# One projection for B, C and the step sizes, and state 2's product with B on GpSimd with its decay in PSUM, in a selective-scan kernel

## The chip, the cores and the metric

The kernel runs on one core of a Trainium2 chip. The metric is the device time of one execution in microseconds (us). A core has five engines that run side by side, each through its own list of instructions in order: TensorE (PE in the profile, its weight loads PEld), VectorE (DVE), ScalarE (ACT), GpSimd (POOL) and SyncE (SP), which here only issues the transfers (DMA) between the memory (HBM) and the on-chip memory (SBUF). PSUM is the second on-chip memory, into which TensorE writes its results.

## The reference

A network of four layers works on four images of 64 x 64 points with 96 channels. Each layer is a token mixer followed by a small feed-forward part in 8-bit floats. Layer 0 has a gated scan of its own; the change does not touch it. Layers 1 to 3 have a mixer that is a selective scan over four orders of the points (rows and columns, forward and backward). With 192 inner channels and 16 states, its core is

```python
delta = softplus(dt_proj(x_dbl[:6]) + dt_bias)      # step sizes
B, C = x_dbl[6:22], x_dbl[22:38]                    # x_dbl = x_proj_weight @ u
dA = exp(delta * A)                                 # decay, A = -(1..16)
h = dA * h + (delta * u) * B                        # for each channel and state, along the 4096 points
y = sum over states of h * C  (+ u * D)
```

All of it is fp32 in the reference.

## The kernel before, in words

**Tiling.** A stage is one image in one layer; layers 1 to 3 with four images make 12 stages, run by `scans`. A stage goes through two directions, four segments of T = 1024 points each, and three chunks of 128 rows (64 channels of one order and 64 of another): 24 chunks, 288 in all. Each chunk has 16 tiles, one for each state, so there are 4608 tiles of 128 x 1024 fp32. A tile is one round of the loop `for k in range(last + 5)`.

**A tile's work.** The decay `da` is an exponential on ScalarE (`decays`), two rounds ahead, in one of three SBUF buffers. The B rows of the state come onto all 128 partitions by two bf16 matmuls with a selection matrix (`b_rows`), one round ahead, in one of two PSUM buffers `bc` (two banks each, from `wide`). `scan` multiplies them by `du` = delta * u on VectorE, in place in PSUM, lets some side work be issued (`beside`), and runs the recurrence on VectorE as one scan instruction into one of three `h` buffers. One round later GpSimd multiplies `h` by the C rows (`times_c`, the result in `c`). Three rounds later TensorE adds the result to the chunk's sum in PSUM (`accumulate`). The C rows come from a small array `cs` in HBM: `c_rows` issues two transfers of 256 KB, each one row spread over 64 partitions, two rounds ahead, into one of six `c` buffers. A buffer is free again when its accumulation is done.

**A segment's preparation** (`next_segment`, `prepare_segment`). The inputs `u` are loaded, and then a projection gives B, C and the six inputs of the step size for two orders at once. The columns of its weights `xp` are B three times over (NB3 = 96), the step inputs (12) and C (32): XPW = 140, more than the 128 partitions of a result. So it is made in two passes, `x_proj_b` (108 rows) and `x_proj_c` (32 rows), each in two halves of 512 points and of three matmuls a half. B is kept as a sum of three bf16 parts in `bs`: the first part is a rounded copy, a VectorE subtraction gives the remainder, ScalarE rounds that, and GpSimd takes the last difference. That is why B stands three times in the projection: each part lies on partitions of its own. The C rows are copied out and stored to `cs`.

**A chunk's preparation** (`prepare_chunk`). While a chunk's 16 tiles run, the next chunk's step sizes are made: matmuls, then a softplus out of ScalarE tables and three GpSimd operations of 128 x 1024, and a fourth on GpSimd for `du`.

**What sets the order.** Every engine runs its instructions in the order in which the program issues them (class `InOrder`); waits between engines are put in from the data's dependences and from buffers that come free. The preparations are Python generators (`Chain`), and each round's `beside` moves each one step on. With one step in each round, and with the chunk's chain begun at state 0, the softplus operations on GpSimd are issued in the rounds of states 5, 8, 11 and 13. Two PSUM banks are shared by the chains and the side job.

**The side job.** The work between two stages (feed-forward, normalisation, the input projection, the 3 x 3 convolution of the next image) is a `Job` whose chains advance by `rate` steps a round, and which is finished by force, if need be, in the second last chunk of the stage at state 4, tile 356 of the stage's 384, where the next stage's first segment begins to load.

```python
            if k + 2 <= last:
                c_rows(k + 2)
                decays(k + 2)
            if n == 11:
                logarithms()
            if k + 1 <= last:
                b_rows(k + 1)
            if 0 <= k - 1 <= last:
                times_c(k - 1)
            if k <= last:
                scan(k, beside)
```

Of the kernel before, what the change touches and what calls it, by code (L numbers as in the profile page):

```python
# [23 lines left out]
R = 6  # L24
HID = 4 * C
# [14 lines left out]
XPW = NB3 + 2 * R + NC2  # L40
# [59 lines left out]
def metaformer(ctx: ExitStack, tc: tile.TileContext, x, l0_ab, l0_rest, ssm, ffn, out):  # L100
# [662 lines left out]
    def load_segment(item):  # L763
# [8 lines left out]
        sg.cs = dram.tile([NC2, T], F32, tag="cs", name="cs")  # L772
        return sg

    def prepare_segment(item, sg):

        xp = weights[item.layer].xp
        m = NB3 + 2 * R

        def project(ps, a, b, k):  # L780

            for c in range(3):
                o = (3 * item.d + c) * XPW
                cols = slice(k * MM, (k + 1) * MM)
                pe.matmul(
                    ps[0 : b - a],
                    xp[:, o + a : o + b],
                    sg.us[c][:, cols],
                    start=c == 0,
                    stop=c == 2,  # L790
                )
                if c:
                    yield

        sg.rows = sb(1, "rows", [128, T])
        for k in range(2):
            cols = slice(k * MM, (k + 1) * MM)
            ps = bank("x_proj_b")
            yield from project(ps, 0, m, k)

            bs = sg.bs[:, cols]
            act.copy(sg.rows[NB3:m, cols], ps[NB3:m])
            sg.steps = k == 1
            act.copy(bs, ps[0:NB3])
            yield
            rem = sg.rows[0:NB3, cols]
            dve.tensor_tensor(rem, ps[0:NB3], bs, ALU.subtract)
            release()
            yield
            for p in (32, 64):  # L810
                act.copy(bs[p : p + 32], rem[p : p + 32])
            yield k == 0
        pool.tensor_tensor(sg.bs[64:96], sg.rows[64:96], sg.bs[64:96], ALU.subtract)
        for k in range(2):
            cols = slice(k * MM, (k + 1) * MM)
            yield True
            ps = bank("x_proj_c")
            yield from project(ps, m, m + NC2, k)
            act.copy(sg.rows[0:NC2, cols], ps[0:NC2])
            release()  # L820
        yield
        sp.dma_start(out=sg.cs, in_=sg.rows[0:NC2])
# [50 lines left out]
    def scans(stages, jobs, pac):  # L873
# [27 lines left out]
        def c_rows(k):  # L901
            i, n = tiles[k]
            c = live[k, "c"] = sb(6, "c", [128, T])
            for half in range(2):
                row = NS * half + n
                sp.dma_start(
                    out=c[64 * half : 64 * half + 64],
                    in_=i.sg.cs[row : row + 1, :].to_broadcast([64, T]),
                )

        def decays(k):
            i, n = tiles[k]
            da = live[k, "da"] = sb(3, "da", [128, T])
# [80 lines left out]
        start(items[0])  # L994
        c_rows(0)
# [449 lines left out]
```

## Time and profile before

| what | value |
|---|---|
| time, median of 3 runs | 19,610.84 us (19,587.28 to 19,634.19) |
| the profiled execution's own time | 19,605.71 us |
| its span, first to last instruction | 19,603.9 us |
| VectorE busy | 17,669.3 us (90%) |
| TensorE busy | 16,279.3 us (83%), granted clock 0.816 |
| GpSimd busy | 15,496.4 us (79%) |
| ScalarE busy | 12,248.8 us (62%) |
| transfers (queue 1) | 3178 MB, 61.6% of the 16 DMA engines' time |
| scan, 128 x 1024, x4608 | 2343 ns each |
| VectorE product `bc<-du,bc`, x4608 | 1208 ns each |
| GpSimd product `c<-h,c`, 128 x 1024, x4608 | 2360 ns each |
| selection matmul `bc<-bs,sel`, x9216 | 457 ns each |
| second projection pass `x_proj_c`, x1152 | 687 ns each |
| row load `c<-cs`, 256 KB, x9216 | 4.2 us from issue to landing |

In a line of groups, the first part is line, engine and operation, then what is written and read (by the program's names) and how often; after it the busy time in us and the mean of one in ns; last the idle time of the engine just before these instructions, and what ended most of it. Nearly every instruction has the line L78, since a helper records them all; so groups go by the names of the tiles. In a list of waits each line says who waited for whom, for how long in total, how often, and the longest. In a list in order of time, the first two numbers are the start and the duration in us. An fp32 matmul leaves two records, a bf16 one leaves one.

### The profile page before, as it was taken

The page shows a single profiled execution, that of the slowest core. Times are in us where ns is not written, and L with a number is a line of the kernel's source. Part 1 is how long each engine was busy: PE and PEld are TensorE (multiplying, and loading weights), DVE is VectorE, ACT ScalarE, POOL GpSimd, SP SyncE. Part 2 cuts the span into 40 slices and gives each one's busy share as a digit, 9 for nine tenths or more (in the row PEclk, how much of TensorE's full clock was granted, in tenths as well). Part 3 has the DMA queues.
Part 4 walks back from the last instruction along what each step waited for, and adds up shares of the span by engine and source line. Part 5 has one row for each costly group of instructions (what it writes and reads, how often), then busy time and mean ns, then how long its engine had stood idle before and what let it go on. Part 6 is the DMA issues. An engine that isn't in the chain of part 4 may idle for free. (4 is left out here: it accounts for less than half of the span.)

```text
span 19603.9 us, 224830 instructions
## 1 busy us (share of the span) xinstructions
PE 16279.3 (83%) x70400; PEld 4745.4 (24%) x70400; DVE 17669.3 (90%) x13768; ACT 12248.8 (62%) x19341; POOL 15496.4 (79%) x10086
## 2 busy tenths in 40 slices
PE   8998787787888888887888887887888888888877
PEld 3332121121122222222222222222222222223223
DVE  6757999999999999999999999999999999998885
ACT  4544665665665665675665665665675665666665
POOL 3435888888888888888888888888888888888886
PEclk9998786787787787797797797797797797797776
DMA  2213666676666666667666667666666666676664
GB/s 52 50 47 89 166 184 168 168 188 166 169 186 172 170 182 180 167 185 182 169 183 180 167 182 183 167 182 182 168 186 178 168 185 176 171 185 171 168 177 115
DMA packets 1269876, 3192.65 MB, mean 163 GB/s; under 512 B 440336, under 2 KB 440560, under 8 KB 1262544
## 3 DMA queue, kind: packets, MB, share of 16 engines
q1 hardware_dynamic: 1268688, 3178.27, 61.6%
q8 instruction: 568, 9.31, 0.2%
q14 instruction: 620, 5.08, 0.1%
HBM read 2818.81 MB, written 308.28 MB: 160 GB/s over the span
## 5 line engine op out<-in xcount | busy, mean ns | idle before, releaser
L78 POOL TENSOR_TENSOR c<-h,c 128x1024 f32<-128x1024 f32 (+1 forms) x4992 | 11332.9, 2276 | 3284.9 <-DVE h L78 1396.4
L78 DVE TENSOR_TENSOR_SCAN h<-da,carry,bc 128x1024 f32<-128x1024 f32 x4608 | 10797.5, 2343 | 598.7 <-POOL c L78 80.8
L78 PE MATMUL acc<-c,twice 64*64 64x512 f32 x36864 | 6246.6, 755 | 57.4 <-POOL c L78 57.4
L78 ACT ACTIVATE da<-delta,decay 128x1024 f32<-128x1024 f32 x4608 | 5280.8, 1148 | 1372.5 <-DVE h L78 1359.7
L78 DVE TENSOR_TENSOR bc<-du,bc 128x1024 f32<-128x1024 f32 x4608 | 5567.1, 1208 | 417.8 <-PE bc L78 389.6
L78 PE MATMUL bc<-bs,sel 96*128 96x512 bf16 x9216 | 3398.6, 457 | 2393.3 <-DVE h L78 2296.6
L78 ACT COPY carry<-h 128x1 f32<-128x1 f32 x3456 | 649.1, 188 | 2997.7 <-DVE h L78 2992.8
L78 PEld LDWEIGHTS <-sel 96*128 96x128 bf16 x9216 | 557.0, 101 | 7376.4 <-DVE h L78 5607.2
L78 PEld LDWEIGHTS acc<-c,twice 64*64 64x64 f32 x36864 | 1131.3, 153 | 2848.4 <-issue 1927.6
L78 ACT ACT_TABLE_LOAD x1165 | 1494.7, 1283 | 36.3 <-DVE mv L78 20.0
L78 PE MATMUL conv<-pad,tap_lo 128*128 128x512 f32 x1728 | 913.5, 639 | 0.6 <-ACT zh L78 0.6
L78 PE MATMUL dt_proj<-rows,w 12*128 12x512 f32 x1152 | 829.5, 807 | 6.3 <-ACT delta L78 6.3
L78 ACT ACTIVATE du<-e,ones 128x1024 f32<-128x1024 f32 x576 | 659.4, 1145 | 202.9 <-POOL delta L78 197.8
L78 POOL TENSOR_TENSOR delta<-delta,du 128x1024 f32<-128x1024 f32 x288 | 679.2, 2358 | 121.7 <-ACT du L78 121.3
L78 PE MATMUL x_proj_c<-u,xp 128*32 128x512 f32 x1152 | 657.8, 687 | 133.2 <-ACT rows L78 125.0
L78 PE MATMUL x_proj_b<-u,xp 128*108 128x512 f32 x1152 | 696.1, 722 | 53.7 <-ACT u L78 12.8
L78 ACT COPY y<-acc 128x1024 f32<-128x1024 f32 x288 | 291.3, 1012 | 713.8 <-PE acc L78 708.9
L78 POOL TENSOR_TENSOR e<-e,du 128x1024 f32<-128x1024 f32 x288 | 679.7, 2360 | 2.4 <-ACT du L78 2.4
L78 POOL TENSOR_TENSOR du<-delta,u 128x1024 f32<-128x1024 f32 x288 | 680.0, 2361 | 0.1
L78 POOL TENSOR_TENSOR delta<-delta,e 128x1024 f32<-128x1024 f32 x288 | 678.7, 2357 | 0.1
L78 ACT ACTIVATE c<-c,l_bias 128x512 f32<-128x512 f32 x384 | 263.6, 686 | 662.6 <-PE c L78 659.8
L78 PE MATMUL conv<-pad,tap_hi 128*128 128x512 f32 (+1 forms) x1152 | 598.8, 621 | 3.8 <-ACT u L78 3.8
(152 smaller groups left out, 15323.9 us busy)
## 6 DMA issues: line engine op xcount, KB each, us to landing
c<-cs SPq DMA_DIRECT2D x9216, 256.0 KB, 4.2
u<-u SPq DMA_DIRECT2D x288, 512.0 KB, 6.8
y<-y SPq DMA_DIRECT2D x1152, 128.0 KB, 3.5
y<-y SPq DMA_DIRECT2D x144, 512.0 KB, 6.4
xr<-x SPq DMA_DIRECT2D x224, 192.0 KB, 5.1
u<-u SPq DMA_DIRECT2D x288, 128.0 KB, 2.7
pad<-y SPq DMA_DIRECT2D x288, 128.0 KB, 5.1
z<-zl SPq DMA_DIRECT2D x96, 256.0 KB, 3.4
```

The costliest lines, as they stand in the source:

```text
L78: ins = f(*a, **k).ins
```

## The change

- The projection has one pass of 108 columns: B once (32), C (32), 32 columns of zeros, and the step inputs (12). One copy brings all rows to SBUF; the remainder of B goes where the zeros were (partitions 64 to 95), and both later parts are rounded from there. `cs` now holds B and C, 64 rows.
- For the tiles of state 2 (`ON_POOL`), the B rows are loaded from `cs` by two transfers into a `c` buffer (`pool_rows`, four rounds ahead), and GpSimd multiplies them by `du` (`times_b`, issued two rounds ahead, in the round of state 0). VectorE has only the scan for that tile, and TensorE no selection matmul.
- The decay of these tiles is written into a PSUM buffer `bc`, one round ahead instead of two.
- The side job's rate is 1.6 steps a round instead of 1.65.

```diff
+ON_POOL = (2,)
...
-XPW = NB3 + 2 * R + NC2
+XPW = NB3 + 2 * R
...
     def prepare_segment(item, sg):
...
+        rows = sg.rows = sb(1, "rows", [128, T])
+        for k in range(2):
+            cols = slice(k * MM, (k + 1) * MM)
+            ps = bank("x_proj")
             for c in range(3):
                 o = (3 * item.d + c) * XPW
                 pe.matmul(
+                    ps[0:XPW], xp[:, o : o + XPW], sg.us[c][:, cols], start=c == 0, stop=c == 2
                 )
                 if c:
                     yield
...
-            act.copy(sg.rows[NB3:m, cols], ps[NB3:m])
+            act.copy(rows[0:XPW, cols], ps[0:XPW])
             sg.steps = k == 1
-            act.copy(bs, ps[0:NB3])
-            yield
-            rem = sg.rows[0:NB3, cols]
-            dve.tensor_tensor(rem, ps[0:NB3], bs, ALU.subtract)
+            act.copy(bs[0:32], ps[0:32])
+            yield
+            rem = rows[64:96, cols]
+            dve.tensor_tensor(rem, ps[0:32], bs[0:32], ALU.subtract)
             release()
             yield
             for p in (32, 64):
-                act.copy(bs[p : p + 32], rem[p : p + 32])
+                act.copy(bs[p : p + 32], rem)
             yield k == 0
-        pool.tensor_tensor(sg.bs[64:96], sg.rows[64:96], sg.bs[64:96], ALU.subtract)
-        for k in range(2):
-            cols = slice(k * MM, (k + 1) * MM)
-            yield True
-            ps = bank("x_proj_c")
-            yield from project(ps, m, m + NC2, k)
-            act.copy(sg.rows[0:NC2, cols], ps[0:NC2])
-            release()
-        yield
-        sp.dma_start(out=sg.cs, in_=sg.rows[0:NC2])
+        sp.dma_start(out=sg.cs, in_=rows[0 : 2 * NC2])
+        pool.tensor_tensor(sg.bs[64:96], rows[64:96], sg.bs[64:96], ALU.subtract)
...
+        def from_rows(i, dst, at):
+
             for half in range(2):
-                row = NS * half + n
+                row = NS * half + at
                 sp.dma_start(
-                    out=c[64 * half : 64 * half + 64],
+                    out=dst[64 * half : 64 * half + 64],
                     in_=i.sg.cs[row : row + 1, :].to_broadcast([64, T]),
                 )
...
+        def on_pool(k):
+            return k <= last and tiles[k][1] in ON_POOL
+
+        def pool_rows(k):
+            i, n = tiles[k]
+            b = live[k, "b"] = sb(6, "c", [128, T])
+            from_rows(i, b, n)
+
+        def times_b(k):
+            i, b = tiles[k][0], live[k, "b"]
+            pool.tensor_tensor(b, i.du, b, ALU.mult)
...
-            da = live[k, "da"] = sb(3, "da", [128, T])
+            da = live[k, "da"] = wide() if on_pool(k) else sb(3, "da", [128, T])
...
-            dve.tensor_tensor(b, i.du, b, ALU.mult)
+            if not on_pool(k):
+                dve.tensor_tensor(b, i.du, b, ALU.mult)
             beside()
...
             if k + 2 <= last:
                 c_rows(k + 2)
-                decays(k + 2)
+                if not on_pool(k + 2):
+                    decays(k + 2)
+            if on_pool(k + 1):
+                decays(k + 1)
+            if on_pool(k + 4):
+                pool_rows(k + 4)
             if n == 11:
                 logarithms()
-            if k + 1 <= last:
+            if k + 1 <= last and not on_pool(k + 1):
                 b_rows(k + 1)
             if 0 <= k - 1 <= last:
                 times_c(k - 1)
+            if on_pool(k + 2):
+                times_b(k + 2)
             if k <= last:
                 scan(k, beside)
...
-                jobs[-1].append(Job(between(im, layer - 1), 1.65))
+                jobs[-1].append(Job(between(im, layer - 1), 1.6))
...
-                for s in range(3):
-                    v[:, 32 * s + NS * order : 32 * s + NS * order + NS] = t[:, R : R + NS]
+                v[:, NS * order : NS * order + NS] = t[:, R : R + NS]
+                v[:, NC2 + NS * order : NC2 + NS * order + NS] = t[:, R + NS :]
                 v[:, NB3 + R * order : NB3 + R * order + R] = t[:, :R]
-                v[:, m + NS * order : m + NS * order + NS] = t[:, R + NS :]
```

More of the change, by code (lines that the diff above doesn't have):

```diff
@@ L771, in load_segment @@
         sg.bs = sb(2, "bs", [NB3, T], BF16)
-        sg.cs = dram.tile([NC2, T], F32, tag="cs", name="cs")
+        sg.cs = dram.tile([2 * NC2, T], F32, tag="cs", name="cs")
         return sg
@@ L777, in prepare_segment @@
         xp = weights[item.layer].xp
-        m = NB3 + 2 * R
-        def project(ps, a, b, k):
+        rows = sg.rows = sb(1, "rows", [128, T])
+        for k in range(2):
+            cols = slice(k * MM, (k + 1) * MM)
+            ps = bank("x_proj")
             for c in range(3):
                 o = (3 * item.d + c) * XPW
-                cols = slice(k * MM, (k + 1) * MM)
                 pe.matmul(
[L786 to L790, printed above, removed]
+                    ps[0:XPW], xp[:, o : o + XPW], sg.us[c][:, cols], start=c == 0, stop=c == 2
                 )
@@ L793, in project @@
                     yield
-        sg.rows = sb(1, "rows", [128, T])
-        for k in range(2):
-            cols = slice(k * MM, (k + 1) * MM)
-            ps = bank("x_proj_b")
-            yield from project(ps, 0, m, k)
             bs = sg.bs[:, cols]
-            act.copy(sg.rows[NB3:m, cols], ps[NB3:m])
+            act.copy(rows[0:XPW, cols], ps[0:XPW])
             sg.steps = k == 1
-            act.copy(bs, ps[0:NB3])
+            act.copy(bs[0:32], ps[0:32])
             yield
-            rem = sg.rows[0:NB3, cols]
-            dve.tensor_tensor(rem, ps[0:NB3], bs, ALU.subtract)
+            rem = rows[64:96, cols]
+            dve.tensor_tensor(rem, ps[0:32], bs[0:32], ALU.subtract)
             release()
@@ L810, in prepare_segment @@
             for p in (32, 64):
-                act.copy(bs[p : p + 32], rem[p : p + 32])
+                act.copy(bs[p : p + 32], rem)
             yield k == 0
-        pool.tensor_tensor(sg.bs[64:96], sg.rows[64:96], sg.bs[64:96], ALU.subtract)
-        for k in range(2):
-            cols = slice(k * MM, (k + 1) * MM)
-            yield True
-            ps = bank("x_proj_c")
-            yield from project(ps, m, m + NC2, k)
-            act.copy(sg.rows[0:NC2, cols], ps[0:NC2])
-            release()
-        yield
-        sp.dma_start(out=sg.cs, in_=sg.rows[0:NC2])
+        sp.dma_start(out=sg.cs, in_=rows[0 : 2 * NC2])
+        pool.tensor_tensor(sg.bs[64:96], rows[64:96], sg.bs[64:96], ALU.subtract)
     def prepare_chunk(item):
@@ L903, in c_rows @@
             c = live[k, "c"] = sb(6, "c", [128, T])
+            from_rows(i, c, NC2 + n)
+        def from_rows(i, dst, at):
             for half in range(2):
-                row = NS * half + n
+                row = NS * half + at
                 sp.dma_start(
-                    out=c[64 * half : 64 * half + 64],
+                    out=dst[64 * half : 64 * half + 64],
                     in_=i.sg.cs[row : row + 1, :].to_broadcast([64, T]),
                 )
+        def on_pool(k):
[7 more added lines that the diff above has]
+            pool.tensor_tensor(b, i.du, b, ALU.mult)
         def decays(k):
             i, n = tiles[k]
-            da = live[k, "da"] = sb(3, "da", [128, T])
+            da = live[k, "da"] = wide() if on_pool(k) else sb(3, "da", [128, T])
             at = (3 * i.d + i.chunk) * NS + n
@@ L994, in scans @@
         start(items[0])
+        for k in range(4):
+            if on_pool(k):
+                pool_rows(k)
+        for k in range(2):
+            if on_pool(k):
+                times_b(k)
         c_rows(0)
@@ L1365, in _scan @@
     xp = np.zeros((128, 2, 3, XPW), np.float32)
-    m = NB3 + 2 * R
     for d in range(2):
```

## The prediction

> **What bounds the kernel now.** I read the page first: busy shares, then the groups, then waits by engine, then single instructions in order of time.
>
> ```profile
> PE 16279.3 (83%) x70400; PEld 4745.4 (24%) x70400; DVE 17669.3 (90%) x13768; ACT 12248.8 (62%) x19341; POOL 15496.4 (79%) x10086
> ...
> L78 POOL TENSOR_TENSOR c<-h,c 128x1024 f32<-128x1024 f32 (+1 forms) x4992 | 11332.9, 2276 | 3284.9 <-DVE h L78 1396.4
> L78 DVE TENSOR_TENSOR_SCAN h<-da,carry,bc 128x1024 f32<-128x1024 f32 x4608 | 10797.5, 2343 | 598.7 <-POOL c L78 80.8
> ...
> L78 DVE TENSOR_TENSOR bc<-du,bc 128x1024 f32<-128x1024 f32 x4608 | 5567.1, 1208 | 417.8 <-PE bc L78 389.6
> ```
>
> VectorE is fullest. 4608 tiles (288 chunks of 16 states) each cost it one product with B and one scan. The list in order of time, in a quiet stretch of the sixth stage, gives the rhythm (start, duration, engine, what):
>
> ```profile
> 9005.56 1.21 DVE L78 TENSOR_TENSOR bc<-du,bc 128x1024 f32<-128x1024 f32 x1
> ...
> 9006.67 1.99 PE L78 MATMUL acc<-c,twice 64*64 64x512 f32 x8
> 9006.90 2.35 DVE L78 TENSOR_TENSOR_SCAN h<-da,carry,bc 128x1024 f32<-128x1024 f32 x1
> 9009.16 1.21 DVE L78 TENSOR_TENSOR bc<-du,bc 128x1024 f32<-128x1024 f32 x1
> 9009.28 1.15 ACT L78 ACTIVATE da<-delta,decay 128x1024 f32<-128x1024 f32 x1 [2.45 <-DVE h L78]
> ...
> 9009.38 2.37 POOL L78 TENSOR_TENSOR c<-h,c 128x1024 f32<-128x1024 f32 x1 [1.25 <-DVE h L78]
> ```
>
> Product to product is 3.60 us: 1.34 from the product's start to the scan's, 2.26 from there to the next product. The median of all 4607 intervals is 3.604, so most tiles run at VectorE's own pace. The products and scans run from 1802 to 19388 us, 17,585 us in all; 4607 x 3.603 = 16,599 of that. The other 986 are the projections' and the side job's VectorE work and real waits. Who VectorE waited for in that stretch:
>
> ```profile
> DVE bc L78 <- PE bc L78: 389.6, 271, 5.1
> DVE h L78 <- POOL c L78: 80.8, 36, 12.5
> DVE x L78 <- PE out_proj L78: 31.0, 20, 2.9
> ```
>
> Its idle time there is 1116 us, of which 599 is the 0.13 between product and scan; real waits are some 517, mostly for TensorE's B rows. GpSimd is busy 14,969 of the 17,585 us, 85.1%. And the SyncE queue:
>
> ```profile
> SPq L78 <- PE acc L78: 9566.6, 3839, 23.0
> ...
> POOL c L78 <- DMA c<-cs: 295.3, 80, 13.6
> ```
>
> The first line: the load of the C rows of a tile waits for the accumulation that frees one of the six "c" buffers. The second: GpSimd sometimes waits for those rows.
>
> **What the Trainium skill says.** "SBUF — State Buffer", section "Who interferes with whom": a VectorE instruction with two SBUF inputs locks out a GpSimd one that reads SBUF; with at most one it doesn't. The trace agrees for one: scans (decay in SBUF, B in PSUM) take 2.31 to 2.35 us from the 1st to the 99th percentile with GpSimd 85% busy beside them. With B in SBUF, the decay in PSUM keeps it at one, so I add no lock. "PSUM — Partial Sum Buffer", "The four PSUM rules": GpSimd cannot touch PSUM; hence B must come to SBUF by DMA for GpSimd's product. "GPSIMD Engine Reference", 3.1: a two-input fp32 product is 1.96 times as slow as on VectorE; here 2360/1208 = 1.95. "ScalarE: Activation LUTs", "Step-by-step", says writing PSUM has the lower latency; no run here shows a decay written there, so I take 1.15 us as now.
>
> **The change part by part** (against the profiled 19,605.7 us: span 19,603.9 and 1.8 around it).
>
> *State 2's product leaves VectorE.* Its tile then costs the scan's 2.26 us in place of 3.60: 288 x 1.34 = **-386 us**. The scan's inputs trade places between SBUF and PSUM, one of each as before, so its duration stays at 2343 ns; were its start 0.07 us worse or better, that is 20 us either way.
>
> *The same product comes to GpSimd:* 288 x 2.36 = 680 us. Share: (14,969 + 680)/(17,585 - 386) = 91%, so it isn't the bound on average; what counts is where it lands. It is issued in the round of state 0, after the previous state 15's product with C. I measured how far GpSimd is from holding up VectorE: a scan needs the "h" buffer of three scans ago, so the margin is from the end of the product with C of tile k to the start of scan k+3. Its median is 5.97 us for states 0 to 4, with a 5th percentile of 4.9 to 5.7 for states 0 to 3, but 0.64 and 0.04 at states 4 and 5. The four softplus sums run in the rounds of states 5, 8, 11 and 13. A delay of 2.36 fits into the 5.97 and is worked off at some 1.2 us a tile (3.60 - 2.36) before state 5, less the job's work and the 1.34 by which state 2's tile is shorter. What rides through to states 4 and 5 costs VectorE directly.
>
> *Its B rows come by DMA:* two issues of 256 KB for each chunk, 576 beside 9216. On SyncE they stand after state 0's C rows and before state 1's, and take one of the six "c" buffers from the round of state 14 to scan 2. The rows wait for the accumulation of state 11, which ends 11.1 us (median) after its own scan; with 0.1 to issue, 0.54 for the second half and 4.3 to land, they are there at 16.0, and GpSimd turns to them at about 16.8. At the 95th percentile they are 0.6 late, while scan 2 would wait only from some 2.5 us of lateness: some 8 us in sum over the 288. Behind them C rows of states 1 to 4 have five buffers instead of six, so they are issued 3 to 5 us later. I put that delay on each one's margin from landing to use (medians 5.4 to 6.9 now): 0 to 0.3 us is left at the 10th percentile of the worst states, and the shorter tile takes up to 1.34 more. So GpSimd will wait 0.5 to 1.5 us in perhaps a third of these tiles. VectorE sees this only where GpSimd is already late (states 4 and 5): I take **+70 us** for this and the product together; between 0 (all inside the 5.97) and 220 (some 0.75 us a chunk).
>
> *The decay goes to PSUM, and is issued one round later,* behind the decay of state 3. From the trace: its end would be 1.20 us (median) before scan 2 needs it; late in 16 of 288 chunks, 5.4 us in sum: **+5**. It takes a "bc" buffer that the B rows of state 2 no longer need, freed by the same scan.
>
> *State 2's selection matmuls go:* 576 x 0.457 us of TensorE, and VectorE's idle time ahead of these products, 20 us in the trace: **-20**.
>
> *One projection:* the C half goes (1152 matmul records, 657.8 us busy), with its two copies of 560 ns and a chain of six steps, which held one of two spare PSUM banks twice; the copy of 12 rows becomes one of 108 (as long: 579 against 582 ns for 96). VectorE's remainder stays one instruction of 677 ns. It runs in the third chunk of a segment; there VectorE's idle time before products of states 4 to 9 is 170 us, against 70 and 33 in the other two chunks. Half of the difference to their mean (170 - 52 = 118): **-60**; between 0 (the side job fills the place) and -120. The row store doubles to 256 KB but leaves some six rounds earlier; nobody waits for it.
>
> *The job's rate 1.65 to 1.6.* The job's last store falls at tile 339 of a stage's 384 (347 in the two that start a layer): 339 x 1.65 = 559 rounds, 347 x 1.65 = 573. At 1.6 they end at tiles 350 and 358; at 356 the kernel finishes a job by force and loads the next segment, whose rows then wait on SyncE for the stores. Two stages of nine can meet that: **+10**, at most 60.
>
> Sum: -386 + 70 + 5 - 20 - 60 + 10 = -381; 19,605.7 - 381 = 19,225. The median of the runs is 19,610.8, 5 above the profiled one: **19,230 us**, 1.9% less.
>
> **The rivals.**
> *Half is given back* (23%): the late C rows make GpSimd late at states 4 and 5, where the softplus sums begin and VectorE already stalls in 5% of chunks. For it: margins of 0.04 to 0.64 there, and GpSimd at 91%. Against: GpSimd's lateness there comes from waits, and extra work ahead of a wait disappears in it. At 0.6 to 0.8 us a chunk more than I took, 170 to 230 us: about 19,400.
> *TensorE's relief is larger* (7%): of the 390 us that VectorE waits for B rows a half goes, 135 more than I took: about 19,090. For it: TensorE loses some 920 us of 16,279. Against: chunks without the C projection wait too.
> *Slower* (7%): the C rows' ring becomes the bound from state 15 to state 4. With five buffers a row set is issued about 4 us into a round, lands 4.9 later, and is needed 9.5 after that round's start: 0.5 us to spare. If loads with the added traffic (62% DMA now, some 65% then) land over 6 us later than that in most chunks, GpSimd's 5.97 is used up and each chunk pays more than the 1.34 it saves. At 0.3 us a chunk over it: 19,700. Against: 95% of loads for states 0 to 3 land within 5.6 us of their second issue.
> *The change does nothing* (3%): VectorE waits at state 3 for B rows as long as it saved at state 2: 19,610. Against: TensorE's work in between is shorter too.
>
> **How the numbers follow.** The main case has 60%: 19,150 to 19,310. Adding most of the half-gain case and of the relief gives 19,100 to 19,450, some 83%. Within 0.2% (39 us, about what a measurement of this kernel can tell from no change) 3%; faster 90%; slower 7%.
>
> **What would show it.** Right: 4320 products on VectorE, 288 more on GpSimd at 2.36; product to product 3.60 except at state 2, where the scan follows the last one by 2.26; VectorE's waits for GpSimd under 150 us; fewer for B rows; C row loads still issued 0.1 us after an accumulation. Wrong: scans over 2.35 us at state 2 (a lock or a slower PSUM read), GpSimd waiting far over 295 us for rows with VectorE waiting behind it, or TensorE's waits unchanged.

## The result and the profile after

| | before | after |
|---|---|---|
| median | 19,611.6 us (4 runs, 19,587 to 19,634) | 19,493.3 us (4 runs, 19,488 to 19,501) |
| profiled execution, its span | 19,605.7, 19,603.9 us | 19,495.1, 19,493.3 us |
| granted TensorE clock | 0.816 | 0.792 |

The ratio is 0.9939 [0.9924, 0.9954]: 118 us or 0.6% faster, against a forecast of 380 us. The sign was right; the time lies 43 us above the upper end of the range.

The page after the change, busy shares and the groups that answer to those shown of before (columns as there):

```profile
PE 15921.6 (82%) x68672; PEld 4667.3 (24%) x68672; DVE 17372.0 (89%) x13480; ACT 12078.4 (62%) x19150; POOL 16126.3 (83%) x10374
...
L79 POOL TENSOR_TENSOR c<-h,c 128x1024 f32<-128x1024 f32 (+1 forms) x4992 | 11307.5, 2276 | 2575.6 <-DMA c<-cs 643.4 <-DVE h L79 581.9 <-ACT c L79 569.8
L79 DVE TENSOR_TENSOR_SCAN h<-da,carry,bc 128x1024 f32<-128x1024 f32 x4320 | 10121.9, 2343 | 608.4 <-POOL c L79 135.7 <-ACT da L79 16.6 <-POOL part_c L79 4.5
...
L79 DVE TENSOR_TENSOR bc<-du,bc 128x1024 f32<-128x1024 f32 x4320 | 5223.2, 1209 | 527.5 <-PE bc L79 502.4 <-POOL carry L79 20.7 <-POOL c L79 0.3
...
L79 POOL TENSOR_TENSOR c<-du,c 128x1024 f32<-128x1024 f32 x288 | 679.7, 2360 | 42.8 <-DMA c<-cs 32.9 <-PE acc L79 7.1 <-PE dt_proj L79 2.4
...
L79 DVE TENSOR_TENSOR_SCAN h<-bc,carry,c 128x1024 f32<-128x1024 f32 x288 | 670.4, 2328 | 47.1 <-ACT bc L79 39.0 <-POOL c L79 2.8 <-POOL bs L79 2.2
```

The operations are what was foreseen: 288 products on GpSimd at 2360 ns, and the scans of state 2, with decay in PSUM and B in SBUF, at 2328 ns, no longer than the others at 2343. VectorE's busy time fell by 297 us, but the span by only 111. The rest is idle time, and the waits of VectorE say for what (waiting engine and tile, the one waited for; us in total, times, longest):

```profile
DVE bc L79 <- PE bc L79: 502.4, 383, 7.2
...
DVE h L79 <- POOL c L79: 139.2, 38, 12.2
...
DVE h L79 <- ACT bc L79: 39.0, 20, 4.2
```

It waits 113 us longer than before for B rows from TensorE (389.6 before), 58 longer for GpSimd (81.5 before), and 39 for the decay in PSUM. GpSimd's wait for rows from HBM more than doubled, from 295.3:

```profile
POOL c L79 <- DMA c<-cs: 676.3, 275, 18.7
```

A table by state, worked out from the trace, shows where this falls. The upper half is the mean time from the start of the previous tile's scan to this one's; the lower half is VectorE's idle time in gaps over 0.16 us (the 0.13 between product and scan left out), summed over the 288 chunks as far as they belong to a tile (627 and 845 us in the whole stretch):

| state | 0 | 1 | 2 | 3 | 4 | 5 | 6 | 7 to 15 | all |
|---|---|---|---|---|---|---|---|---|---|
| interval before, us | 3.80 | 3.72 | 3.72 | 3.70 | 3.86 | 3.86 | 3.83 | 34.57 | 61.06 |
| interval after, us | 3.90 | 3.74 | 2.59 | 3.74 | 4.20 | 4.05 | 3.98 | 34.47 | 60.67 |
| idle before, us | 32 | 17 | 21 | 17 | 52 | 59 | 53 | 368 | 619 |
| idle after, us | 41 | 27 | 69 | 44 | 142 | 100 | 101 | 311 | 835 |

State 2 is 1.13 us shorter; states 3 to 6 together give 0.72 of it back. (The mean of a state is drawn up by a few long waits; the median is 3.60 us before and after at nearly every other state, and 2.26 at state 2 after.) A list in order of time shows one chunk in which that happens (start, duration, engine, operation; in brackets the idle time before it and what ended it). It begins with the scan of state 2:

```profile
9088.33 2.32 DVE L79 TENSOR_TENSOR_SCAN h<-bc,carry,c 128x1024 f32<-128x1024 f32 x1
...
9090.58 1.21 DVE L79 TENSOR_TENSOR bc<-du,bc 128x1024 f32<-128x1024 f32 x1
...
9091.89 2.35 DVE L79 TENSOR_TENSOR_SCAN h<-da,carry,bc 128x1024 f32<-128x1024 f32 x1
...
9093.83 1.98 PE L79 MATMUL acc<-c,twice 64*64 64x512 f32 x8
...
9095.75 1.04 PE L79 MATMUL bc<-bs,sel 96*128 96x512 bf16 x2
...
9096.82 1.23 DVE L79 TENSOR_TENSOR bc<-du,bc 128x1024 f32<-128x1024 f32 x1 [2.59 <-PE bc L79]
...
9100.91 2.35 POOL L79 TENSOR_TENSOR c<-h,c 128x1024 f32<-128x1024 f32 x1 [4.20 <-DMA c<-cs]
...
9103.47 1.23 DVE L79 TENSOR_TENSOR bc<-du,bc 128x1024 f32<-128x1024 f32 x1 [2.94 <-PE bc L79]
```

The scan of state 2 follows at once and the tile of state 3 too. Then VectorE stands for 2.59 us: the selection matmuls of state 4 stood on TensorE behind the matmuls of the next chunk's step sizes (2.07 us), the side job's transposes and the 64 x 64 accumulations. From 9090 to 9104 us the record has TensorE busy for 14.00 of 14 us at a mean clock of 0.53. The next stop, 2.94 us, ends with TensorE too. GpSimd has just waited 4.20 us for C rows, but the accumulation that needs its product comes only after the B rows here, so this stop is not its doing.

### The profile page after: what moved, and what is told of

Read it like the earlier page. It is cut to its first block, busy times and chain, and to the rows that moved or that the text cites. A ratio compares the mean times of both kernels' runs of the same rounds, so it can differ in the third digit from the quotient of the medians.

```text
span 19493.3 us, 222532 instructions
## 1 busy us (share of the span) xinstructions
PE 15921.6 (82%) x68672; PEld 4667.3 (24%) x68672; DVE 17372.0 (89%) x13480; ACT 12078.4 (62%) x19150; POOL 16126.3 (83%) x10374
## 4 chain that ended last, share of the span: by engine, by line
DVE 44%; PE 21%; ACT 15%; POOL 7%; issue 5%; DMA 5%; SPq 2%; DVEq 0%; POOLq 0%; ACTq 0%
DVE h L79 31%; DVE bc L79 11%; PE acc L79 5%; ACT da L79 5%; PE bc L79 5%; POOL c L79 4%; DMA c<-cs 3%; PE conv L79 3%; ACT L79 2%; PE dt_proj L79 2%; SPq L79 2%; PE y_t L79 1%; ACT du L79 1%; POOL delta L79 1%; PE c L79 1%
## 5 line engine op out<-in xcount | busy, mean ns | idle before, releaser
L79 DVE TENSOR_TENSOR_SCAN h<-da,carry,bc 128x1024 f32<-128x1024 f32 x4320 | 10121.9, 2343 | 608.4 <-POOL c L79 135.7
L79 PE MATMUL acc<-c,twice 64*64 64x512 f32 x36864 | 6400.4, 775 | 108.8 <-POOL c L79 78.2
L79 DVE TENSOR_TENSOR bc<-du,bc 128x1024 f32<-128x1024 f32 x4320 | 5223.2, 1209 | 527.5 <-PE bc L79 502.4
L79 ACT ACTIVATE da<-delta,decay 128x1024 f32<-128x1024 f32 x4320 | 4952.2, 1148 | 1062.8 <-DVE h L79 1051.5
L79 PE MATMUL bc<-bs,sel 96*128 96x512 bf16 x8640 | 3256.3, 466 | 2588.7 <-DVE h L79 2441.9
L79 PEld LDWEIGHTS acc<-c,twice 64*64 64x64 f32 x36864 | 1178.4, 158 | 3038.6 <-issue 1966.2
L79 PE MATMUL dt_proj<-rows,w 12*128 12x512 f32 x1152 | 893.2, 865 | 32.9 <-ACT delta L79 29.9
L79 PE MATMUL x_proj<-u,xp 128*108 128x512 f32 x1152 | 717.7, 739 | 74.9 <-DMA u<-u 32.0
L79 POOL TENSOR_TENSOR delta<-delta,du 128x1024 f32<-128x1024 f32 x288 | 679.8, 2360 | 114.2 <-ACT du L79 112.6
L79 POOL TENSOR_TENSOR c<-du,c 128x1024 f32<-128x1024 f32 x288 | 679.7, 2360 | 42.8 <-DMA c<-cs 32.9
L79 DVE TENSOR_TENSOR_SCAN h<-bc,carry,c 128x1024 f32<-128x1024 f32 x288 | 670.4, 2328 | 47.1 <-ACT bc L79 39.0
```

The lines of the kernel that those rows point to most:

```text
L79: ins = f(*a, **k).ins
```

## The experiments

Two theories stood against each other first. **T**: TensorE, which runs at a lower clock after the change, can't deliver B rows faster than it did, so the time saved at state 2 is waited off. **R**: the loads into the ring of six `c` buffers (used in turn, so that a load waits until the buffer of six loads back is free) make the C rows late, GpSimd with them, and then everything that waits for GpSimd. The parts of the change are priced by building them one upon another; all ratios are to the kernel before, with their 95% interval. A difference of two ratios is uncertain by some 0.2%, or 40 us.

### The projection and the rate

The projection alone (`e1`), and then with the old rate (`e11`):

```diff
-ON_POOL = (2,)
+ON_POOL = ()
```

> The changed kernel with no state on GpSimd (ON_POOL empty): the one projection and the job's rate 1.6 alone, nothing left out. Before 19,611 us, changed 19,493. Theory T (TensorE, at half its clock for half of the time, is full in rounds 3 to 5 and hands B rows over late, so the 386 us that VectorE saves at state 2 are partly waited away): the projection takes work from TensorE, so 19,540 to 19,600, with VectorE's waits for B rows at or below the 390 us of before. Theory R (rows: the B row loads and the five buffers left for C rows make GpSimd late): the same, 19,540 to 19,600. Theory P (the single pass itself costs time, by its chain steps or by a lower granted clock): over 19,650, which would mean that the state on GpSimd brought its full gain.

Measured: 0.9895 [0.9879, 0.9912], 19,415.7 us. It is faster than the whole change: the part with state 2, as it was made, costs 0.44% or 86 us. Its waits, VectorE's for B rows (389.6 us before) and for GpSimd, and then GpSimd's for C rows:

```profile
DVE bc L79 <- PE bc L79: 275.9, 235, 6.3
...
DVE h L79 <- POOL c L79: 59.3, 25, 13.5
```

```profile
POOL c L79 <- DMA c<-cs: 260.6, 87, 15.7
```

```diff
-                jobs[-1].append(Job(between(im, layer - 1), 1.6))
+                jobs[-1].append(Job(between(im, layer - 1), 1.65))
```

> The projection-only kernel with the side job's rate put back to 1.65, which splits the 1.05% between the two edits. If the projection brings it: ratio 0.989 to 0.992. If the rate does: 0.995 to 0.999. My prediction gave 60 us (0.3%) to the projection and a loss of 10 us to the rate.

Measured: 0.9948 [0.9932, 0.9965], 19,508.3 us. So about half of the gain of `e1` is the rate: the projection at 1.65 brings 0.52%, the step to 1.6 another 0.53%. The idle time of VectorE (gaps over 0.16 us, between the first and the last scan) is 496 us at 1.65 and 402 at 1.6, and at state 10 alone 98 against 18. That fits side-job steps falling on a fuller round at one rate than at the other, but why at that state was not settled. What the rate does with a state on GpSimd was not run.

### What the saved product brings

VectorE's product of state 2 is left out, with everything else of `e1` kept, the selection matmuls too. The scan then reads the B rows without `du`, so the output differs in this state:

```diff
-            if not on_pool(k):
+            if n != 2:
                 dve.tensor_tensor(b, i.du, b, ALU.mult)
```

> The projection-only kernel with VectorE's product of state 2 left out and nothing put in its place: the scan takes the B rows in PSUM as they are; the selection matmuls stay, the decay stays in SBUF. The run with du in the scan lost about 267 of the 386 us between these two. If the removed selection matmuls (a gap in TensorE's activity, then half clock in rounds 3 and 4) are what lost it, this one gains over 250 of 386: below 19,165. If the shorter round alone is what TensorE can't follow, it gains as little as there: about 19,300.

Measured: 0.9813 [0.9799, 0.9828], 19,275.3 us. Against `e1` this is 0.82% or 161 us for 386 us of work taken off VectorE, with nothing put on another engine and no transfer added. VectorE's idle time grew by 192 us (402 to 594), and its wait for B rows from 275.9 to

```profile
DVE bc L79 <- PE bc L79: 383.4, 336, 6.3
```

This is theory T without R: the product alone, gone, already lengthens the wait for TensorE by 107 us, and by another 22 where the scan of state 2 now waits itself for the B rows. At state 2 the interval fell from 3.78 to 2.50; state 4's rose from 3.74 to 4.00. It is T without the lower clock, too: in the rounds of states 3 and 4 the mean clock is 0.83 in `e6` and 0.83 and 0.85 in `e1`.

Next, on the changed kernel, the scan of state 2 reads `du` itself from SBUF, with its decay in PSUM, no selection matmuls, no loads and no product anywhere:

```diff
-            b = live[k, "b"] = sb(6, "c", [128, T])
-            from_rows(i, b, n)
+            live[k, "b"] = None
...
-            pool.tensor_tensor(b, i.du, b, ALU.mult)
+            live[k, "b"] = tiles[k][0].du
```

> The changed kernel without the B row loads and without GpSimd's product: at state 2 the scan reads du itself in place of du * B, so the product with B of that state is left out; the decay is still in PSUM and there are still no selection matmuls. All six row buffers serve C rows again and GpSimd has 680 us less to do. Theory T: TensorE's waits stay, so 19,430 to 19,490, at most 60 us under the changed kernel. Theory R: the lost 200 us and more come back, 19,220 to 19,320.

Measured: 0.9835 [0.982, 0.9849], 19,296.6 us. So with a product that costs nothing at all, the changed kernel would gain some 325 us over the kernel before, of which `e1` has 206 without it. Taking the selection matmuls off and putting the decay into PSUM brought nothing over `e6` (0.22% the other way, at the edge of what the intervals tell apart). VectorE's wait for B rows is longer than in `e6`:

```profile
DVE bc L79 <- PE bc L79: 465.1, 368, 6.3
```

Here the clock is lower, 0.76 and 0.75 in the rounds of states 3 and 4. Were the missing matmuls the trouble, because TensorE then has less to do and is granted a lower clock, two matmuls with zero weights in their place would help (in `accumulate` at state 14, which has its turn in the round in which state 2's selection matmuls are missing):

```diff
+            if n == 14:
+                for j in range(2):
+                    cols = slice(j % 2 * MM, j % 2 * MM + MM)
+                    pe.matmul(i.acc[0:64, cols], zeros, i.sg.bs[:, cols], start=False, stop=False)
```

> The kernel whose state 2 scans du (no loads, no GpSimd product, no selection matmuls: 19,297 us), with two bf16 matmuls of 512 columns with zero weights put where the selection matmuls of state 2 stood (round of state 1, ahead of the accumulation, added into the sum as zeros). Theory clock gate: the activity is back, the granted clock in rounds 3 and 4 returns from 0.76 towards 0.84, and 60 to 150 us are gained: 19,150 to 19,240. Theory plain load (TensorE has too much work in rounds 3 to 5): no gain or a loss, 19,290 to 19,330.

Measured: 0.9813 [0.9797, 0.983], 19,269.2 us, clock 0.804 against 0.795 (0.82 and 0.84 in those two rounds). The gain is 0.22%, at the edge of the intervals, and the wait for B rows is 436 us, still 160 more than in `e1`. So the lower clock is at most a small part.

The round of state 3 also holds a second set of accumulating matmuls, the skip term at the start of each chunk's sum. It was left out (with it `u * D`, or the forward direction's sum, is missing from the output), once with VectorE's product and once without:

```diff
-                if i.d == 0:
-                    add_quarters(i, i.sg.us[i.chunk], weights[i.layer].skip[:, i.chunk, :], True, False)
-                else:
-                    add_quarters(i, i.yf, stacked, True, False)
-            add_quarters(i, h, stacked, False, n == NS - 1)
+            add_quarters(i, h, stacked, n == 0, n == NS - 1)
```

> The projection-only kernel without the four matmuls (eight records) that open each chunk's sum with u * D or with the sums of the other direction, so that part of the output is left out. They run in the round of state 3. It is the reference for the next run: by the trace VectorE waits little for TensorE in rounds 3 and 4 with the projection alone, so ratio 0.984 to 0.990.

> The same with VectorE's product of state 2 left out too, as in the run without product. If TensorE has no room in rounds 3 to 5, the 1 to 2 us taken from it there let the product's 386 us come through: 1.4 to 1.9% below the run before, where it was 0.8% with these matmuls. If the loss lies elsewhere: again 0.7 to 1.0%. If the missing activity lowers TensorE's granted clock as in the light kernels: less than 0.7%.

Measured: 0.9901 [0.9885, 0.9918] and 0.9807 [0.9788, 0.9827]. The product's absence brings 0.94% here and 0.82% with the skip matmuls: the same within the intervals. So that load on TensorE is not what eats the saving. The idle time stays (647 us against 422 in `e17`), the largest part of it at state 4 (112 us).

### TensorE's clock

Three quarters of the accumulating matmuls of states 0 to 14 are left out, before and after the change, so that TensorE has room (the sums then lack those parts):

```diff
-                for j in range(2):
+                for j in range(1 if few else 2):
```

(and the same for the loop over `k`, with `few` true for `n < NS - 1`)

> The kernel before with three quarters of the matmuls of each accumulation left out for states 0 to 14 (one of the four quarters of the sum is added, so that the buffer is still held until TensorE has read it); the sums are incomplete. TensorE loses some 70% of its 6,250 us of accumulations. Theory T: VectorE's 390 us of waits for B rows nearly vanish: 19,200 to 19,300. Theory R: most of it too, since this concerns the kernel before.

> The changed kernel with the same matmuls left out as in the light kernel before. Theory T: with room on TensorE the saving at state 2 arrives in full: 330 to 400 us under the light kernel before. Theory R: the loads and buffers still make GpSimd late, so the difference between the two light kernels stays near the 118 us of the full ones, at most 200.

Measured: 1.0421 [1.0406, 1.0437] and 1.0272 [1.0256, 1.0287]. Both are slower, with three tenths of these matmuls; the 292 us between the two lie between what T and R forecast. The matmul group of `e3` shows why, and then its wait of VectorE:

```profile
L78 PE MATMUL acc<-c,twice 64*64 64x512 f32 x10944 | 7173.7, 890 | 40.5 <-POOL c L78 40.5
```

```profile
DVE bc L78 <- PE bc L78: 1105.2, 798, 5.7
```

10,944 records keep TensorE as busy as 36,864 did (6246.6 us before). The four quarters overlap: before, those records last 755 ns each, 27,800 us in all, in 6246.6 us of busy time. So leaving out three of four saves little. And the clock fell, as the views of the core's clock say for before and for `e3`:

```profile
die 0 (median of its cores): 19603.9 us, clock 0.816
```

```profile
die 0 (median of its cores): 20449.0 us, clock 0.695
```

So the pair didn't take load off TensorE and says nothing between T and R. It goes with what a low clock would cost: the selection matmuls take 519 ns in place of 457, and the wait for B rows is nearly three times as long. The reverse, on `e1`: two zero-weight matmuls ahead of every accumulation.

```diff
+            if True:
+                for j in range(2):
+                    cols = slice(j % 2 * MM, j % 2 * MM + MM)
+                    pe.matmul(i.acc[0:64, cols], zeros, i.sg.bs[:, cols], start=False, stop=False)
```

> The projection-only kernel with the same two zero-weight matmuls ahead of every accumulation, 9216 more matmuls on TensorE and nothing left out. Theory clock gate: more activity keeps the clock up, from 0.80 to over 0.88, and VectorE's waits for TensorE (276 us) fall: 19,150 to 19,350. Theory plain load: each costs 0.2 to 0.4 us on an engine that is already late: 19,500 to 19,900.

Measured: 1.0039 [1.0024, 1.0054], 1.4% slower than `e1`, at a clock of 0.92 in place of 0.80. The accumulations became shorter (666 ns in place of 771; 5472 us in all in place of 6394), but the fillers took more than that, 0.33 us each (groups of `e8`):

```profile
L79 PE MATMUL acc<-c,twice 64*64 64x512 f32 x36864 | 5472.2, 666 | 22.3 <-POOL c L79 22.3
L79 PE MATMUL acc<-bs,zeros 96*64 96x512 bf16 x9216 | 3058.8, 416 | 0.0
```

### The ring of `c` buffers

On `e1`, which has no use for them, the B rows of state 2 are loaded as the change does, held until the round of state 3, and read by one small ScalarE copy:

```diff
+        def hold_rows(k):
+            b = live[k, "hold"] = sb(6, "c", [128, T])
+            from_rows(tiles[k][0], b, tiles[k][1])
+
+        def drop_rows(k):
+            act.copy(scrap, live.pop((k, "hold"))[:, 0:1])
...
+            if n == 3 and (k - 1, "hold") in live:
+                drop_rows(k - 1)
...
+            if k + 4 <= last and tiles[k + 4][1] == 2:
+                hold_rows(k + 4)
```

> The projection-only kernel (19,416 us) with state 2's B rows loaded into a row buffer from the round of state 14 until scan 2, as in the changed kernel, but used by nothing (a copy of one column, 0.2 us on ScalarE, ends their life); VectorE still makes the product. Nothing is left out. It prices the loads and the five buffers alone. Theory R: 100 to 200 us slower than the projection alone. Theory T, now in the form that TensorE's granted clock, which follows its activity, decides: at most 40 us.

Measured: 1.0010 [1.0002, 1.0019], 19,655.7 us: 1.15% slower than `e1`. VectorE's and then GpSimd's waits, between the first and the last scan:

```profile
DVE bc L79 <- PE bc L79: 359.4, 294, 6.3
DVE h L79 <- POOL c L79: 127.2, 31, 14.0
```

```profile
POOL c L79 <- DMA c<-cs: 538.3, 192, 17.6
```

GpSimd's wait was 260.6 us in `e1` over the same stretch: the held rows alone double it. Besides the two waits of VectorE shown there is a third that grew, for the rows `xr` that the side job loads through the same SyncE queue, from 10.0 us in `e1` to

```profile
DVE st L79 <- DMA xr<-x: 59.3, 16, 6.7
```

Now the parts, each alone. First the hold without the traffic (64 bytes in place of 512 KB), then the traffic without the hold (the buffer given back at once, the copy reads something else):

```diff
-            from_rows(tiles[k][0], b, tiles[k][1])
+            sp.dma_start(out=b[0:1, 0:16], in_=tiles[k][0].sg.cs[0:1, 0:16])
...
-            act.copy(scrap, live.pop((k, "hold"))[:, 0:1])
+            act.copy(scrap[0:1], live.pop((k, "hold"))[0:1, 0:1])
```

> As the run with rows held, but only 64 bytes are loaded into the row buffer in place of 512 KB, so the buffer is taken from the round of state 14 to scan 2 (and SyncE waits for it in the same place) without the traffic. Holding cost some 225 us over the projection alone (ratio to the kernel before 1.001 against 0.9895). If the five buffers (and the SyncE queue that stands still behind them) are the cause: 0.997 to 1.002. If the traffic is: 0.989 to 0.993.

```diff
-            act.copy(scrap, live.pop((k, "hold"))[:, 0:1])
+            act.copy(scrap, ones)
+            live.pop((k, "hold"))
```

> As the run with rows held, with the full two loads of 256 KB for each chunk, but the buffer is given back as soon as they have landed (the 0.2 us copy on ScalarE stays, on another source). The traffic and SyncE's wait for the buffer stay, the hold from landing to scan 2 goes. If the hold is the cause: ratio 0.990 to 0.995; if the traffic or the wait at state 14 is: 0.997 to 1.002.

Measured: 0.9995 [0.9986, 1.0004] and 1.0002 [0.9996, 1.0009]. Either alone costs about as much as both. What they share is the small copy and the place that the buffer takes in the ring's turn. The copy alone, and then, with that copy, the loads into another buffer, `e`, of the softplus, which is idle in that part of the chunk:

```diff
-            b = live[k, "hold"] = sb(6, "c", [128, T])
-            from_rows(tiles[k][0], b, tiles[k][1])
+            live[k, "hold"] = None
```

> The projection-only kernel with only the 0.2 us ScalarE copy that the three runs with rows held or loaded had in common, 288 of them, and neither buffer nor load. If the copy were the cause of their 210 us: ratio 0.998 to 1.001. If the ring or the loads are: as the projection alone, 0.988 to 0.991.

```diff
-            b = live[k, "hold"] = sb(6, "c", [128, T])
+            b = live[k, "hold"] = sb(1, "e", [128, T])
```

> The same copy and the full two loads of 256 KB at state 14, but into the buffer e, which the softplus chain has finished with by then; the six row buffers serve C rows alone. If the ring of six is the cause: 0.988 to 0.992. If the traffic is: 0.997 to 1.001.

Measured: 0.9891 [0.9875, 0.9908] (the copy is free) and 0.9927 [0.9912, 0.9942]: the traffic as such costs 0.36%, some 70 us, and the turn in the ring 1.04%, some 200 us, without the traffic (`e9` against `e13`) and 0.75 to 0.83%, some 155 us, with it (`e10` and `e5` against `e14`). The two don't simply add up. The trace shows how the turn costs: with six buffers in use by turns, the load for tile k is issued 0.1 us after the accumulation of tile k - 6. One tile taken in between, and the loads of states 1 to 4 are issued 0.1 us after that of tile k - 5, in the changed kernel, in `e9`, and also in `e10`, whose extra buffer is free again at once but is not used before its turn. In the changed kernel that is 2.2 to 5.7 us (median) later than the accumulation of tile k - 6. From the traces:

| state of the C rows | 1 | 2 | 3 | 4 |
|---|---|---|---|---|
| margin from landing to GpSimd's product, median, before, us | 6.7 | 6.9 | 5.4 | 6.3 |
| the same after | 4.1 | 1.9 | 1.9 | 1.0 |

Under 0.3 us of margin, so that GpSimd waited or nearly did, had 0, 3 and 5% of the rows of states 2, 3 and 4 before, and 26, 19 and 31% after. Of the 348 us by which the waits of GpSimd's products with C for rows grew, 174 fall on states 1 to 4 and 147 on state 7, whose load is issued 1.3 us (median) after the accumulation of tile k - 6, in place of 0.3; that part is not explained.

### Another state, and a better version

The same change at state 12, in place of 2:

```diff
-ON_POOL = (2,)
+ON_POOL = (12,)
```

> The changed kernel with state 12 on GpSimd in place of state 2: the product is issued in the round of state 10, the rows are loaded from the round of state 8, and the short round comes where TensorE has room (it is busy for 72 to 81% of rounds 11 to 13 with the projection alone, against 90 to 94% of rounds 2 to 4). Theory T (TensorE can't follow the short round at state 2): over 100 us faster than the changed kernel, ratio 0.985 to 0.990. Theory R (the loads and the hold): no better than it, 0.992 to 0.999, and worse where the softplus operations of states 8 and 11 meet the product.

Measured: 0.9976 [0.9964, 0.9988], 19,578.1 us, slower than at state 2. So T's forecast, that TensorE's room at this state lets the saving through, failed, and R's came. VectorE's idle time is 958 us, of it 206 at state 14 and 110 at state 12, against 23 and 4 in `e1`; it waits 548 us for B rows and 205 for GpSimd. Since this kernel takes the turn in the ring too, it can't tell what the place alone is worth.

Last, the change with its buffers chosen by the experiments: the B rows go into `e`, and GpSimd writes the product into the `da` buffer that state 2's decay no longer needs. Nothing is left out.

```diff
-            b = live[k, "b"] = sb(6, "c", [128, T])
+            b = live[k, "b"] = sb(1, "e", [128, T])
...
-            pool.tensor_tensor(b, i.du, b, ALU.mult)
+            live[k, "b"] = sb(3, "da", [128, T])
+            pool.tensor_tensor(live[k, "b"], i.du, b, ALU.mult)
```

> The changed kernel with the B rows loaded into e and GpSimd's product written into the da buffer that state 2 leaves free since its decay is in PSUM; nothing left out. If the ring is the cause: near the run that scans du (ratio 0.9835) plus what GpSimd's product costs, 0.983 to 0.988, faster than the projection alone (0.9895). If traffic or GpSimd's lateness is: 0.992 to 0.996, as the changed kernel.

Measured: 0.9842 [0.9827, 0.9857], 19,322.4 us: 1.6% faster than the kernel before, 1.0% faster than the changed one, and 0.07% from `e2`, which has no product at all. Its waits of VectorE, and of GpSimd:

```profile
DVE bc L79 <- PE bc L79: 475.1, 379, 6.3
...
DVE h L79 <- POOL c L79: 80.9, 32, 12.5
```

```profile
POOL c L79 <- DMA c<-cs: 301.5, 84, 13.6
```

GpSimd's waits for rows and VectorE's for GpSimd are back at the values of before (295.3 and 81.5), with all 288 products on GpSimd. What stays is T's: 475.1 us for B rows from TensorE, nearly the 465.1 of `e2`. With `e7`'s two filler matmuls a chunk added:

> The same with the two zero-weight matmuls of the filled run in the place of state 2's selection matmuls. The filler gained 0.2% on the run that scans du; if it does here: 0.981 to 0.986. If TensorE has no room for it: equal or slower by up to 0.2%.

Measured: 0.9849 [0.9835, 0.9864], 19,337.4 us, no different, though the clock in the rounds of states 3 and 4 rose from 0.74 and 0.73 to 0.80 and 0.81.

## Why the prediction was right and wrong

Both theories hold, each for its own part. The differences between the ratios above, taken of 19,620 us, against the terms of the prediction's sum. Each measured term is uncertain by some 40 us, and holds for the order in which the parts were built one upon another:

| term | predicted, us | measured, us | from |
|---|---|---|---|
| state 2's product leaves VectorE | -386 | -161 | `e6` against `e1` |
| GpSimd's product and its loads, outside the ring | +70, with the next | +14 | `e15` against `e2` |
| their turn in the ring | | +190 | changed kernel against `e15` |
| decay in PSUM, selection matmuls gone | -15 | +43 | `e2` against `e6` |
| one projection | -60 | -102 | `e11` |
| rate 1.6 | +10 | -104 | `e1` against `e11` |
| sum | -381 | -120 | |

**The step that failed is "*State 2's product leaves VectorE*".** It counted the whole 288 x 1.34 us, because VectorE is the fullest engine and most tiles run at its pace. The durations were right (the interval at state 2 is 2.50 us in `e6`), but a round shortened on VectorE brings its next product sooner, and then the B rows of the following states are what ends last: the waits for them grew from 3, 15 and 51 us at states 3, 4 and 5 in `e1` to 44, 75 and 59 in `e6`, and TensorE was never idle for over 0.16 us in these waits or in the 2 us before them. The busy share of TensorE in the rounds of states 2, 3 and 4, from scan to scan, was 0.93, 0.90 and 0.91 in the trace of before, against 0.83 over all: a number that was there to be read stage by stage, and wasn't. The rival *The change does nothing* named this wait and this state, and had 3%; its argument against itself, that TensorE's work in between is shorter too, failed, since `e2` without the selection matmuls does no better. In size that rival was wrong too: the 161 us remain. Which part of TensorE's work would have to move for the other 225 us is open: not the missing matmuls (`e7`), not the skip term (`e18`). In the two profiled executions the loss is 204 us; 192 of it are seen as idle time on VectorE, 130 of that as waits for B rows. The rest is spread over waits for ScalarE, GpSimd and loads of under 16 us each.

One rival was not run. In `e6` TensorE itself waited long for VectorE, before the selection matmuls:

```profile
PE bc L79 <- DVE h L79: 2387.9, 2072, 4.7
```

With two `bc` buffers it can make the B rows of a tile only after the scan two tiles back. At states 3 to 5 its own list is what ended last, as said, but with a third buffer it might have worked ahead there. Whether that would bring back the lost time is not shown.

**"*Its B rows come by DMA*" had the mechanism right and the price wrong.** Five buffers for states 1 to 4 and loads issued later (2.2 to 5.7 us, foreseen 3 to 5) are in the trace. GpSimd waits there less often than foreseen but longer: in 143 of 1152 tiles, 2.4 us each, where the prediction had a third of them and 0.5 to 1.5 us. But it was costed at +70 with GpSimd's product, on the ground that GpSimd's lateness is hidden behind 5.97 us of margin up to state 4. The runs give 190 for the turn in the ring and 14 for the product and its loads (`e14` gives 70 for the loads alone, on another kernel: the small terms are not sharp).

The margin counted only the scan that waits for `h`. With the held rows alone (`e5`) VectorE's wait for GpSimd is 68 us longer than in `e1` (127.2 against 59.3), that for B rows 84 longer, and that for the side job's rows 49 longer: together 201 of the 225 us that they cost. A late product is also a late accumulation (TensorE waits 76 us for GpSimd there, in place of 32), and the B rows stand in the same list behind it; and a load that waits for its buffer holds up the side job's loads behind it on SyncE. That these two paths explain the 84 and the 49 is argued from the order of the lists, not shown by a run of its own. The rival *Half is given back* had this cause, late C rows, and a figure of 170 to 230 us for it: right in cause and size, though it saw only the waits for GpSimd, and it was added to a main term that was itself too large.

**The decay and the selection matmuls**: the wait for the decay was put at 5.4 us and is 39.0 in the trace, 20 waits, the longest 4.2; the selection matmuls brought nothing that shows. Their common +43 is at the edge of the intervals. *TensorE's relief is larger* failed: with the projection and the rate VectorE's wait for B rows fell by 114 us (`e1`), but with state 2 it is longer than before, and TensorE's busy time fell by 358 us where that rival counted 920.

**The projection** was taken as half of 118 us; it brought 102. **The rate** was priced by its forced finish alone (+10, at most 60) and has the other sign: minus 104 us. That term had no view behind it for what a rate does in the rounds themselves. So the sign of the whole came right by luck: the terms of state 2, for which the change was forecast to be faster, add up to +86 us, and the two small terms beside them brought 156 us more than forecast.

**GpSimd's product**, the point about which the prediction worried most, was the one that cost next to nothing: GpSimd is at 83% of the span and takes 288 more products without a loss that shows, once its rows are on time. (In the prediction's share, 14,969 us is the sum of GpSimd's records, which overlap a little; its busy time in that stretch was 14,734. The 1.96 that the Trainium skill gives in "GPSIMD Engine Reference", 3.1, was measured on an addition of 2048 columns; this product, of 1024, takes 1.95 times as long as on VectorE. That GpSimd cannot touch PSUM was tested by no run here.) *Slower*, the ring as the bound, is half true: as built, the part with state 2 costs 86 us over the projection alone.

## What to carry to other kernels

What a shorter instruction on the fullest engine brings can stop short at the next engine's room in the same rounds: read that engine's busy share and the waits for it there, before counting the saving whole. A tile taken out of turn from a full ring of buffers puts off the tiles behind it, here those of four states, even if it is given back at once; look for a buffer that is idle at that time, which here was worth 1.0%. And a change of several parts is measured part by part: here a rate altered in passing and a smaller projection brought 1.05%, while the part that gave the change its name lost 0.44% until its buffers were moved.

## What the runs showed of the hardware

Less work on TensorE went with a lower clock, and the work that was left took longer. The second projection pass took 658 us away, but TensorE's busy time fell by only 302 in `e1` (15,977 from 16,279): the accumulations grew from 6247 to 6394 us, the selection matmuls from 3399 to 3497. The records of the clock hold two values only, 1.0 and 0.5, in steps of 3.41 us. Between the first and the last scan the half clock held for 38.5% of the time before and 43.6% after; in the rounds of states 3 and 4, those behind the missing selection matmuls, the mean fell from 0.85 to 0.73. The Trainium skill says in "TensorE: Matmul & The Clock Gate", "Part 1: The HAM clock gate (the "warmup" mystery)": the default state is throttled, and activity within windows of about 3.4 us releases the throttle. The traces agree: with seven tenths of the accumulating records gone the clock is 0.695, with fillers 0.92. What was not expected is that neither direction paid in this kernel, with TensorE 82% busy: the low clock of `e3` goes with a time 4.2% longer, and the high clock of `e8`, bought with 3059 us of fillers, with one 1.4% longer than `e1`'s.

A 64 x 64 quarter alone occupied TensorE about as long as four side by side: 7174 us for 10,944 records at a clock of 0.695, 6247 us for 36,864 at 0.816. And an exponential written into PSUM took 1103 ns, one into SBUF 1148.
